# Late expert slots appended to the early slots' chain, and the residual stream's stores moved to another queue and one step later

## The chip, the cores and the metric

The kernel runs on one core of a Trainium2 chip. Its time is the device time of one execution, in microseconds (us). Each core has five engines that run their own instruction streams: TensorE (PE, matmuls), VectorE (DVE), ScalarE (ACT), GpSimd (POOL) and SyncE (SP). Data moves by DMA; a transfer is issued by one of the engines' queues, here mostly the synchronous engine's (SP) and GpSimd's, and all of them share the same 16 DMA engines. An engine takes its instructions in order, so one that waits for a semaphore holds everything behind it on that engine.

## What is computed

The reference is a two-layer decoder over 4 batches of 512 tokens of width 256. The last two stages are what the change touches. Stage five is a cross attention block with its own feed-forward network; stage six is a mixture of experts, 8 experts with 1024 hidden units, of which each token takes the best two:

```python
gate_scores = jax.nn.softmax(x @ Wg + bg, axis=-1)
topk_scores, topk_idx = jax.lax.top_k(gate_scores, TOP_K)
topk_scores = topk_scores / (jnp.sum(topk_scores, axis=-1, keepdims=True) + 1e-08)
...
for e in range(NUM_EXPERTS):
    h = jax.nn.gelu(x @ W1[e] + b1[e])
    y = h @ W2[e] + b2[e]
    output = output + y * combine_w[..., e:e + 1]
```

The input x of this stage is a layer norm of the residual stream, and the stage's output is added to the residual stream.

## The kernel before

**The expert stage.** The kernel does not multiply every token with every expert. For each batch `gate` computes the layer norm, the gate scores and the best two experts, and scatters every token's normalised row (256 values and four more for its weights and its number) to two places in a tensor `rows` in device memory, where each expert has its own region: eight indirect DMAs of 128 rows each, on GpSimd's queue (L1667). It also adds the experts' second biases to the residual stream (`biases2`, VectorE L1687) and, in its last piece, stores that batch of the residual stream to the tensor `sums` (L1689, GpSimd's queue).

The rows of an expert are then worked off in slots of 128 rows; there are 39 slots. For a slot, the synchronous queue loads the 128 rows (`zs`, L1791) and the whole weights of its expert (`we`, 2 MB, L1797). `turn` transposes the rows on TensorE (L1812), copies them on VectorE (`zsT`, L1814) and computes the tokens' numbers (`to`, L1818) and weights (`wts`, L1820 and L1821). `hidden` makes the hidden units in two halves of 16 matmul instructions on TensorE (L1830) and the activations on ScalarE (L1832). `output` multiplies with the second weights (L1837), scales on VectorE (`ys`, L1839) and adds the 128 rows to `sums` with an indirect DMA on GpSimd's queue (L1840). At the very end the kernel copies `sums` to its output (L1878).

`sums` is one tensor to the framework that places the waits, so every access to it, a store of a batch or a scatter-add, waits for the one before. The pool of `to` and `wts` has four buffers, so slot k's `to` waits until the scatter-add of slot k - 4 has landed. The pool of `we` has four buffers too, `ys` has three, `zs` has 16.

**Early and late slots.** After the third of the four batches the first 16 slots (`NEARLY`) can be filled from what has been scattered by then; `count_early` and `table_early` decide which expert and which rows each has. The other 23 need the last batch (`count_late`, `table_late`). So early slots start while the last batch's feed-forward part and gate still run.

**Who sets the order.** Stages two, five and six are laid out by a planner, `Stream`, in steps `s.t`. Its attention tiles have fixed steps. Everything else hangs in chains: lists of pieces, each with the step from which it may be laid, the step by which it must be, a gap in steps, a cost and a function that issues its instructions. `fill` lays pieces of any chain that are ready and for which there is room, the one with the earliest due step first; between chains with the same due step the first in the list goes first. A piece with cost 0 has room always. Once attention's tiles are done, the room is 3.0 a step for each of two kinds of cost.

The early slots are one chain, made by `tail` from `slots.begin` (L1296), due at step 10**6. Its rounds are: fetch slot s + 3 (cost 0), `hidden` of slot s + 1 in two halves (2.0 each), `turn` of slot s + 2 (0.5), `output` of slot s (3.4). A fetch of a slot loads `zs` (late slots only; the early ones' are all loaded at the beginning) and `we`; slot 16 loads `we` first. The late slots are a second chain with the same due step, made by `rest` (L1435) among the gate's pieces of the last batch. Its first piece is the fetch of slot 16, with cost 0, so it is laid as soon as the chain is there, while the early chain's next piece has no room. The emitted order of loads is therefore slots 0 to 8, then 16, then 9 to 15, then 17 and on. The load of slot 16's table entries waits for `table_late`, and that of its `zs` for the last batch's row scatters.

The gate's pieces for batch b are put together in `gate` and made into a chain by `leave` (L1437), which inserts the counts, the tables, and `slots.go` or `rest` at places counted from the list's end.

Of the kernel before, what the change touches and what calls it, by code (L numbers as in the profile page):

```python
# [20 lines left out]
P = 128  # L21
B, T, C = 4, 512, 256
# [18 lines left out]
def decoder_kernel(ctx: ExitStack, tc: tile.TileContext, a: dict, out: bass.AP):  # L41
    nc = tc.nc
    V, G, S, PE = nc.vector, nc.gpsimd, nc.scalar, nc.tensor

    def ts(i, n=P):
        return slice(i * n, (i + 1) * n)

    def mid_bc(ap, n):
        return ap.unsqueeze(1).to_broadcast([ap.shape[0], n, ap.shape[1]])
# [31 lines left out]
    def ring():  # L81
        return banks["s"].tile([P, 512], F32, name="ps_s", tag="s")
# [132 lines left out]
    def add_to(dst, ps):  # L215
        V.tensor_add(dst, ps, dst)
# [93 lines left out]
    class Stream:  # L310
# [22 lines left out]
        def chain(self, items, spill=False):  # L333
            items = [[*i] for i in items]
            for i, j in zip(items[-2::-1], items[:0:-1]):
                i[1] = min(i[1], j[1])
            self.chains.append(SimpleNamespace(items=deque(items), at=-99, spill=spill))

        def lay(self, c):
            cost, fn = c.items.popleft()[3:]  # L340
            c.at = self.t
            fn()
            if not c.items:
                self.chains.remove(c)
            self.spent[cost < 0] += abs(cost)
# [893 lines left out]
    def l1_xattn(cn_d, moe, early):  # L1239
        with early.stack as st:  # L1240
# [25 lines left out]
            def ffn_weights(p, w):  # L1266
                w["li1"] = load(early.pl, "li1", rows(f"{p}_li1"), [P, 4, C])
                w["li2"] = load(early.pl, "li2", rows(f"{p}_li2"), [P, 2, 1024])
                w["li3"] = load(one, "li3", rows(f"{p}_li3"), [P, 8, C])
# [6 lines left out]
            for k in range(2):  # L1276
# [8 lines left out]
            s = Stream(  # L1285
                list(jobs.values()), tail=lambda: tail(), ptp=ptp, ptmp=wk, op=one, qap=qmp, nms=nms, ones=ones, identb=identb,
                onesf=onesf,
            )

            back = set()  # L1290
            slots = Slots(moe, gs)

            def tail():
                if slots.ready:
                    inner.close()
                    s.chain([(s.t + 4, 10**6, 0, c, f) for c, f in slots.begin(st)])  # L1296
                return slots.ready

            def block(k, b):
# [31 lines left out]
                def flip(z, c, outs):  # L1331
                    ps = ring()
                    for t in range(NT):
                        PE.transpose(ps[:, ts(t)], z[:, t, ts(c)], ident)
                    for n, (dst, o) in enumerate(outs):
                        gc, bc = pv[:, o + c : o + c + 1], pv[:, o + 2 + c : o + 3 + c]
                        if n == 0:
                            S.activation(dst[:, c, :], ps, AF.Identity, bias=bc, scale=gc)
                        else:
                            V.tensor_scalar(dst[:, c, :], ps, gc, bc, ALU.mult, ALU.add)  # L1340
# [56 lines left out]
                def mlp():  # L1397
                    def li1(t):
                        ps = ring()
                        for g in range(4):  # L1400
                            PE.matmul(ps[:, 0:C], e.yT[:, g, ts(t)], w["li1"][:, g, :], start=g == 0, stop=g == 3)
                        add_to(e.xo[:, t, :], ps[:, 0:C])

                    def mid():
                        e.nT = one.tile([P, 2, T], F32, name="nT5", tag="nT5")
                        G.tensor_add(x1, x1, e.xo)
                        G.tensor_add(x1, x1, mid_bc(bl3, NT))

                    def li2(f):
                        if f == 0:  # L1410
                            e.h = one.tile([P, 8, T], F32, name="hT5", tag="hT5")
                        ps = ring()
                        for c in range(2):
                            PE.matmul(ps, w["li2"][:, c, ts(f)], e.nT[:, c, :], start=c == 0, stop=c == 1)
                        if f % 2:
                            S.activation(e.h[:, f, :], ps, AF.Identity, bias=pv[:, 12 + f : 13 + f])
                        else:
                            V.tensor_scalar_add(e.h[:, f, :], ps, pv[:, 12 + f : 13 + f])

                    def gelu():  # L1420
                        S.activation(e.h, e.h, AF.Gelu)
                        S.preload_act_table_set("natural_log_exp_and_others")
                        if k:
                            e.kept = one.tile([P, NT, C], F32, name="kept", tag="xo")
                            nc.sync.dma_start(e.kept, kept[b])

                    def li3(t):
                        ps = ring()
                        for f in range(8):
                            PE.matmul(ps[:, 0:C], e.h[:, f, ts(t)], w["li3"][:, f, :], start=f == 0, stop=f == 7)  # L1430
                        add_to(x1[:, t, :], ps[:, 0:C])

                    def rest():
                        s.chain([(s.t, 10**6, 0, c, f) for c, f in slots.rest()])

                    def leave():
                        if k:  # L1437
                            G.tensor_add(x1, x1, e.kept)
                            g = gate(
                                moe, b, SimpleNamespace(), gs,  # L1440
                                lambda: one.tile([P, 2, T], F32, name="hT6", tag="hT6"), ring,
                            )
                            more = {
                                B - 2: [(1, 1.0, slots.count_early), (1, 1.0, slots.table_early)],
                                B - 1: [(1, 1.0, slots.count_late), (1, 1.0, slots.table_late)],
                            }.get(b, [])
                            g[-7:-7] = more
                            if more:
                                g[-3:-3] = [(0, 0.0, rest if b == B - 1 else slots.go)]
                            s.chain([(s.t, s.t + 2 + int(0.7 * i), gap, c, f) for i, (gap, c, f) in enumerate(g)])  # L1450
                        back.add(b)
                        if not k and b == B - 1:
                            ffn_weights("a2", ws[1])

                    t0 = s.t
                    work = [(True, 1.7, lambda: li1(0))] + [(False, 1.7, lambda t=t: li1(t)) for t in range(1, 4)]
                    work += [(1, -1.2, p) for p in ln_pieces(e.xo, z3)]
                    work += [(0, 0.0, mid), (True, 0.5, lambda: flip(e.z3, 0, [(e.nT, 8)]))]
                    work += [(False, 0.5, lambda: flip(e.z3, 1, [(e.nT, 8)]))]
                    work += [(f == 0, 1.7, lambda f=f: li2(f)) for f in range(8)]  # L1460
                    work += [(True, 0.0, gelu)]
                    work += [(t == 0, 3.4, lambda t=t: li3(t)) for t in range(4)]
                    work += [(False, 0.0, leave)]


                    lag, pace = {(0, 0): (1, 1.0), (0, B - 1): (3, 1.1), (1, B - 2): (2, 0.65)}.get((k, b), (3, 1.0))
                    s.chain([
                        (t0, t0 + (1 if i < 4 else lag + int(pace * (i - (i > 8)))), gap, c, f)
                        for i, (gap, c, f) in enumerate(work)
                    ])  # L1470
# [17 lines left out]
                for g in range(4):  # L1488
                    u = jobs[k, b, g]
                    u.done = lambda o, g=g: finish(g, o)  # L1490
                    f = u.first_d
# [79 lines left out]
    def gate(m, b, e, gs, hT, bank):  # L1571
        xb = x[:, ts(b, NT), :]
# [91 lines left out]
        def scatter(t):  # L1664
            for k in range(2):
                i = b * NT + t
                G.indirect_dma_start(  # L1667
                    m.rows, bass.IndirectOffsetOnAxis(ap=m.idx[:, i, k : k + 1], axis=0), e.zr[:, t, :], None
                )
# [13 lines left out]
        def biases2(h):  # L1683
            ps = bank()
            for t in range(2):
                PE.matmul(ps[:, ts(t, C)], e.cT[:, ts(2 * h + t)], m.b2, start=True, stop=True)
            V.tensor_add(xb[:, ts(h, 2), :], ps.rearrange("p (t c) -> p t c", c=C), xb[:, ts(h, 2), :])  # L1687
            if h:
                G.dma_start(m.sums[ts(b, T), :].rearrange("(t p) c -> p t c", p=P), xb)  # L1689

        return (
            [(2 if i == 0 else 1, -1.2, p) for i, p in enumerate(ln_pieces(xb, z))]
# [1 line left out]
            + [(1, -1.5, choose), (1, -1.2, choose2), (1, -1.2, choose3), (1, 0.5, rank)]  # L1694
            + [(t == 0, 0.0, lambda t=t: scatter(t)) for t in range(NT)]
            + [(1, 0.7, biases), (1, 0.9, lambda: biases2(0)), (0, 0.9, lambda: biases2(1))]
        )


# [312 lines left out]
```

## Time and profile before

| what | us |
|---|---|
| median of 3 runs | 3479.34 |
| lowest and highest run | 3470.84 and 3481.77 |
| the profiled execution's own time | 3483.41 |
| its span | 3481.7 |
| TensorE busy | 3066.6 (88%) |
| VectorE busy | 2092.8 (60%) |
| ScalarE busy | 1902.4 (55%) |
| GpSimd busy | 815.4 (23%) |
| DMA moved | 174.52 MB, mean 50 GB/s |
| first and last scatter-add issued | 3110.4 and 3468.3 |

Times in the profile count from the span's start. A row such as `we<-in_we` names the tile that is written and what it is read from; a line number is that of the kernel before. In a timeline, a row gives the start, the duration, the engine, the line, the operation with its tiles, how many instructions it merges, and in square brackets how long the engine sat idle before it and what released it. DMA rows on GpSimd's queue show the issue, not the landing. SPq is the synchronous engine's queue. In the waits, a row gives the waiting engine and tile, what it waited for, the total in us, how many times, and the longest.

### The profile page before, as it was taken

The numbers are of one execution on the slowest core, as the hardware profiler recorded it, in microseconds if no ns is written. First come the engines' busy times: TensorE is split into PE (matmuls) and PEld (weight loads), VectorE is DVE, ScalarE is ACT, GpSimd is POOL, SyncE is SP. The second block draws the span as 40 slices with busy tenths as digits, with TensorE's granted clock in tenths as the row PEclk, the third lists the DMA queues.
The fourth block names the chain that finished last, engine by engine and source line by source line (L and its number), as shares of the span: only waits on it lengthen the run. The fifth ranks groups of instructions, "written<-read, shape, count | busy, mean of one in ns | idle before, by whom it ended". The sixth has DMA issues, their size and how long they took to land. (4 is left out here: it accounts for less than half of the span.)

```text
span 3481.7 us, 50606 instructions
## 1 busy us (share of the span) xinstructions
PE 3066.6 (88%) x19095; PEld 1497.5 (43%) x19095; DVE 2092.8 (60%) x5138; ACT 1902.4 (55%) x3845; POOL 815.4 (23%) x679
## 2 busy tenths in 40 slices
PE   6689999999998666677899999999999998987997
PEld 3433333334334344344434444433333333447896
DVE  4576676777765687876676565665746646433111
ACT  2225555454554764779588676556663664542221
POOL 1010112122022745668212121100101201122111
PEclk9889999999999567777799999999998999999998
DMA  9100000010001100120000000000000000045896
GB/s 287 55 28 7 1 7 3 6 31 4 10 19 42 49 6 32 37 86 7 25 1 1 1 4 16 7 1 31 13 1 5 21 1 13 13 172 172 288 310 190
DMA packets 78405, 174.52 MB, mean 50 GB/s; under 512 B 5640, under 2 KB 61200, under 8 KB 72976
## 3 DMA queue, kind: packets, MB, share of 16 engines
q1 hardware_dynamic: 68304, 155.47, 12.9%
q0 software_dynamic: 7728, 11.47, 1.5%
q10 hardware_dynamic: 2128, 4.34, 0.3%
q8 instruction: 150, 2.46, 0.3%
q14 instruction: 95, 0.78, 0.1%
HBM read 125.46 MB, written 47.90 MB: 50 GB/s over the span
## 5 line engine op out<-in xcount | busy, mean ns | idle before, releaser
L426 ACT ACTIVATE pt<-ps_s 128x512 f32<-128x512 f32 (+2 forms) x1536 | 792.1, 569 | 744.8 <-PE ps_s L425 649.6
L390 PE MATMUL ps_s<-kT,qT 32*128 32x512 f32 (+3 forms) x3072 | 923.0, 623 | 45.7 <-ACT pt L426 27.9
L402 DVE TENSOR_REDUCE mx<-ps_s 128x1 f32<-128x512 f32 x768 | 489.7, 684 | 221.7 <-PE ps_s L390 123.2
L390 PEld LDWEIGHTS ps_s<-kT,qT 32*128 32x128 f32 x3072 | 309.8, 186 | 338.8 <-issue 96.9
L394 DVE TENSOR_REDUCE mx<-ps_s 128x1 f32<-128x512 f32 x512 | 328.5, 685 | 193.4 <-PE ps_s L390 190.1
L425 PE MATMUL ps_s<-qa,kT 32*128 32x512 f32 (+3 forms) x1536 | 440.5, 588 | 4.5 <-ACT pt L426 3.1
L425 PE MATMUL ps_s<-qT,kT 32*128 32x512 f32 x1536 | 418.6, 638 | 0.0
L406 ACT ACTIVATE ps_s<-ps_s,mx 128x512 f32<-128x512 f32 x512 | 340.8, 670 | 27.5 <-DVE mx L394 27.0
L1832 ACT ACTIVATE hid<-ps_s,we 128x128 f32<-128x128 f32 x312 | 88.9, 368 | 236.4 <-issue 146.1
L1109 POOL TENSOR_TENSOR s<-s,mh 128x1280 f32<-128x1280 f32 x64 | 186.7, 2942 | 81.9 <-ACT mh L1108 64.1
L398 DVE CUSTOM_DVE_ANT_0 junk<-ps_s,dmask 128x256 f32<-128x256 f32 (+3 forms) x256 | 125.6, 491 | 92.0 <-PE ps_s L425 40.3
L1830 PE MATMUL ps_s<-zsT,we 128*128 128x128 f32 x1248 | 153.6, 283 | 26.6 <-DMA we<-in_we 14.8
L167 POOL TENSOR_TENSOR ln_r<-ln_ve,mhalf 128x4 f32<-128x4 f32 x40 | 40.8, 1020 | 532.5 <-DVE ln_ve L162 468.7
L1830 PEld LDWEIGHTS ps_s<-zsT,we 128*128 128x128 f32 x1248 | 150.9, 199 | 32.4 <-issue 17.1
L425 PEld LDWEIGHTS ps_s<-qa,kT 32*128 32x128 f32 x1536 | 143.3, 184 | 47.3 <-DVE mx L402 23.9
L1092 PE MATMUL ps_s<-qk 32*128 32x256 f32 (+3 forms) x512 | 103.2, 609 | 67.2 <-DVE mh L1097 56.5
L418 PE MATMUL ps_s<-qm,all 3*128 3x512 bf16 x768 | 156.9, 388 | 5.9 <-ACT ps_s L406 3.1
L1124 POOL TENSOR_TENSOR s<-s 128x1280 f32<-128x1280 f32 x64 | 147.6, 2337 | 12.3 <-ACT s L1120 12.3
L1151 DVE COPY pt<-ps_s 128x512 f32<-128x512 f32 x160 | 108.4, 688 | 62.0 <-PE ps_s L1149 62.0
L1149 PE MATMUL ps_s<-ident,s 128*128 128x128 f32 x640 | 130.5, 341 | 16.5 <-ACT s L1143 15.3
L1837 PE MATMUL ps_s<-we,hid 128*128 128x256 f32 x624 | 141.7, 381 | 0.0
L1097 DVE TENSOR_SCALAR_CACHE_REDUCE mh<-ps_s 128x512 f32<-128x512 f32 (+3 forms) x256 | 108.5, 487 | 51.7 <-PE ps_s L1096 27.4
(435 smaller groups left out, 5155.1 us busy)
## 6 DMA issues: line engine op xcount, KB each, us to landing
we<-in_we SPq DMA_DIRECT2D x39, 2052.0 KB, 9.1
rows<-zero SPq DMA_DIRECT2D x8, 2080.0 KB, 19.1
qk_d<-qkT SPq DMA_DIRECT2D x32, 256.0 KB, 2.5
qk<-qk_d SPq DMA_DIRECT2D x8, 1024.0 KB, 6.2
zs<-rows SPq DMA_DIRECT2D x39, 130.0 KB, 8.8
li<-in_a_li SPq DMA_DIRECT2D x4, 1024.0 KB, 5.5
v_d<-vp SPq DMA_DIRECT2D x16, 143.5 KB, 1.8
v<-v_d SPq DMA_DIRECT2D x4, 574.0 KB, 6.8
```

The source lines that it names most:

```text
L390: PE.matmul(ps[:, 0:n], u.qT[r, ts(qt)], u.kT[r, hf * 512 : hf * 512 + n], start=True, stop=True)
L394: V.tensor_reduce(m, ps[:, 0:n], AX.X, ALU.max, negate=True)
L402: V.tensor_reduce(m, ps[:, 0:n], AX.X, ALU.max)
L406: S.activation(ps, ps, AF.Exp, bias=m, accum_out=sm)
L418: PE.matmul(ps, self.ones[r, :], u.qm[r, :], start=True, stop=False)
L425: PE.matmul(ps[:, c0:], u.kT[r, ts(kt)], (u.qa if u.first_row else u.qT)[r, c0:], start=u.first_row, stop=True)
L426: S.activation(u.pt[:, j, c0:], ps[:, c0:], AF.Exp, scale=u.scale)
L1109: G.tensor_add(s, s, m)
L1124: G.tensor_mul(s, s, s)
L1149: PE.transpose(ps[:, ts(j)], u.s[h // 2][:, h % 2, c0 : c0 + P], ident)
L1830: PE.matmul(ps[:, ts(f)], u.w[:, k : k + P], u.zT[:, c, :], start=c == 0, stop=c == 1)
L1837: PE.matmul(ps[:, 0:C], u.h[:, f, :], u.w[:, 2048 + f * C : 2048 + f * C + C], start=f == 0, stop=f == 7)
```

## The change

Two things are changed. First, `rest` no longer makes a chain of its own. `Stream.chain` returns the chain that it makes, `tail` keeps it, and `rest` appends the late slots' pieces to it, so that they are laid after the early ones; if the early chain has already run empty, it is put back in the planner's list. Second, the store of a batch of the residual stream is taken out of `biases2` and becomes a piece of its own, `store`, one step later at the earliest. For batches 0 to 2 the synchronous queue issues it; for the last batch GpSimd does, as before. The places that `leave` counts from the list's end are moved by one, so that what it inserts stands where it stood.

```diff
@@ Stream.chain
             self.chains.append(SimpleNamespace(items=deque(items), at=-99, spill=spill))
+            return self.chains[-1]
@@ l1_xattn: tail
                 if slots.ready:
                     inner.close()
-                    s.chain([(s.t + 4, 10**6, 0, c, f) for c, f in slots.begin(st)])
+                    slots.chain = s.chain([(s.t + 4, 10**6, 0, c, f) for c, f in slots.begin(st)])
@@ l1_xattn: block, mlp
                     def rest():
-                        s.chain([(s.t, 10**6, 0, c, f) for c, f in slots.rest()])
+                        c = slots.chain
+                        if not c.items:
+                            s.chains.append(c)
+                        c.items.extend([s.t, 10**6, 0, cost, f] for cost, f in slots.rest())
@@ leave
-                            g[-7:-7] = more
+                            g[-8:-8] = more
                             if more:
-                                g[-3:-3] = [(0, 0.0, rest if b == B - 1 else slots.go)]
+                                g[-4:-4] = [(0, 0.0, rest if b == B - 1 else slots.go)]
@@ gate
             V.tensor_add(xb[:, ts(h, 2), :], ps.rearrange("p (t c) -> p t c", c=C), xb[:, ts(h, 2), :])
-            if h:
-                G.dma_start(m.sums[ts(b, T), :].rearrange("(t p) c -> p t c", p=P), xb)
+
+        def store():
+            (nc.sync if b < B - 1 else G).dma_start(m.sums[ts(b, T), :].rearrange("(t p) c -> p t c", p=P), xb)
...
             + [(1, 0.7, biases), (1, 0.9, lambda: biases2(0)), (0, 0.9, lambda: biases2(1))]
+            + [(1, 0.0, store)]
```

In the emitted order, TensorE, VectorE and ScalarE have the same instructions in the same order as before. GpSimd's queue loses the three stores of batches 0 to 2. The synchronous queue gains them: batch 0's stands between the load of `kept` for batch 0 and the context load (`cn`) of batch 3, batch 1's between the loads of `kept` for batches 1 and 2, batch 2's between the last early `zs` load and slot 3's weights. Slot 16's `we` and `zs` loads stand behind slot 15's `we`.

## The prediction

> **What bounds the kernel now.** I read the page first. TensorE is busy for 88% of the span, but the chain that ended last is not TensorE's: it is one DMA after another.
>
> ```profile
> span 3481.7 us, 50606 instructions
> DMA sums<-ys,to 5%; DVE wts L1821 0%; DVE to L1818 0%; DVE wts L1820 0%; POOLq L2008 0%; DVE ys L1839 0%; POOLq L1840 0%
> sums<-ys,to POOLq DMA_INDIRECT x39, 6.5
> ```
>
> These are the 39 scatter-adds of the expert slots, each adding 128 rows into `sums`. GpSimd issues each one only when the one before has landed. The waits confirm it. The `to` cast of a slot sits on VectorE until the scatter four slots earlier has landed, 30 times, and TensorE's wait for expert weights is small beside that.
>
> ```profile
> DVE to L1818 <- DMA sums<-ys,to: 176.8, 30, 10.3
>   DMA we<-in_we: 14.8, 4
> ```
>
> The second line comes from the view of the tile `we`: four waits of TensorE for weights, 14.8 us in all. I then read the timelines of the tail, GpSimd's first, then TensorE's and the synchronous queue's.
>
> ```profile
> 3208.99 1.61 POOL L1840 DMA_INDIRECT sums<-ys,to  x1 [0.30 <-issue]
> 3214.01 0.84 POOL L1689 DMA_DIRECT2D sums<-x  x1 [3.41 <-DVE wts L1821]
> 3227.36 1.60 POOL L1840 DMA_INDIRECT sums<-ys,to  x1 [12.51 <-DMA sums<-x]
> ...
> 3281.91 1.54 POOL L1840 DMA_INDIRECT sums<-ys,to  x1 [7.50 <-DVE wts L1821]
> ...
> 3362.62 1.54 POOL L1840 DMA_INDIRECT sums<-ys,to  x1 [5.01 <-DVE wts L1821]
> 3371.28 1.54 POOL L1840 DMA_INDIRECT sums<-ys,to  x1 [7.11 <-DVE wts L1821]
> ...
> 3449.01 1.54 POOL L1840 DMA_INDIRECT sums<-ys,to  x1 [5.27 <-DVE wts L1821]
> 3455.00 1.56 POOL L1840 DMA_INDIRECT sums<-ys,to  x1 [4.45 <-DVE ys L1839]
> ...
> 3468.34 1.54 POOL L1840 DMA_INDIRECT sums<-ys,to  x1 [2.94 <-DMA sums<-ys,to]
> ```
>
> The reader sees a chain without a gap from 3209 to the end, and three step lengths. While weights stream at an even pace, 3281.91 to 3362.62 is 11 steps of 7.34 us. Where TensorE stalls and the weight loads come in pairs, 3371.28 to 3449.01 is 9 steps of 8.64. With no weights left, 3455.00 to 3468.34 is 3 steps of 4.45.
>
> ```profile
> 3206.96 3.62 PE L1837 MATMUL ps_s<-we,hid 128*128 128x256 f32 x16
> 3221.54 5.56 PE L1830 MATMUL ps_s<-zsT,we 128*128 128x128 f32 x32 [10.96 <-DMA we<-in_we]
> ...
> 3382.73 5.21 PE L1830 MATMUL ps_s<-zsT,we 128*128 128x128 f32 x32 [2.55 <-DVE zsT L1814]
> ```
>
> ```profile
> 3194.11 0.34 SPq L1797 DMA_DIRECT2D we<-in_we  x1
> 3210.22 0.34 SPq L1791 DMA_DIRECT2D zs<-rows  x1
> 3211.41 1.51 SPq L1797 DMA_DIRECT2D we<-in_we  x2
> ```
>
> TensorE's largest weight wait, 10.96 us, comes from this queue. The load at 3194.11 is slot 16's, the first late slot, issued ahead of slots 9 to 15. Behind it the same slot's `zs` holds the queue until the last batch's row scatters have landed (3210.22), and slot 9's weights start at 3211.41.
>
> **The change part by part.** The profiled execution took 3483.41 us around its span of 3481.7, 0.12% above the median of 3479.34. I work the sum as a difference and apply it to the median.
>
> *Stores of batches 0 to 2 move from GpSimd to the synchronous queue.* Off GpSimd come three issues of 0.82 to 0.84 us and their waits. Batch 0's had no wait and idle time behind it: nothing. Batch 1's held GpSimd for 18.84 us for VectorE's L1687, with L1406 and L1407 behind it. Those feed the third output matrix of that block and the load of `kept` (2966.12), whose reader L1438 starts at 3033.13, so nothing again; without that cover it would be up to 19 us. Batch 2's stood in front of work that TensorE waited for:
>
> ```profile
> 3083.68 0.82 POOL L1689 DMA_DIRECT2D sums<-x  x1
> 3084.52 2.35 POOL L1378 TENSOR_TENSOR xo<-x,bc 128x1024 f32<-128x1024 f32 x1
> ...
> 3087.33 8.22 PE L1401 MATMUL ps_s<-li,yT 128*128 128x256 f32 x26 [7.48 <-POOL yT L1390]
> ```
>
> So `xo`, `yT` and the last block's first output matrix come 3084.52 - 3083.68 = 0.84 us earlier. The gain lies between 0 (a later wait swallows it) and 0.84; nothing in the last block runs beside it as an alternative path, so I take 0.84.
>
> On the synchronous queue the three stores have this cost. Batch 0's now waits for L1687 at 2713 ahead of the context load of batch 3, which went out at 2512.37. That load moves to about 2716, lands in 4.8 us (the median of its row), and its first reader is the key matmul at 2768.8: 48 us of cover. Batch 1's stands ahead of `kept` and is ready at 2963, before that load's own 2966. Batch 2's goes behind the 13 `zs` loads (3113.84) and ahead of slot 3's weights. It delays those by one issue, about 1.1 us by the queue's spacing, but they land near 3124 and TensorE reads them at 3150.76. The first scatter-add must now wait for this store: 3114.9 plus the row's 4.5 us is 3119.4, not 3110.41. Behind it on GpSimd stands L1438 at 3148.07, which waits 36.02 us for VectorE: 28 us of cover. All nothing. Batch 3's store keeps its place on GpSimd between the same two scatter-adds, so its 12.51 us wait stays unless the traffic around it changes.
>
> *Late slots in the early chain.* No instruction is added or removed, and TensorE's, VectorE's and ScalarE's order is unchanged. Slot 16's weights and `zs` move behind slot 15's on the synchronous queue. Slot 9's load goes out at 3194.1; slots 10 and 11 follow outputs 6 and 7 (about 3203.4 and 3210.6). All four weight buffers then serve the next slots, not three. All four weight waits, 14.8 us, should go, with the slow matmuls after the long one (5.56 against 3.73 us): 14.8 + 1.8 = 16.6 us for TensorE.
>
> How much of that reaches the end? TensorE may lead the scatter-adds by about five slots only: slot k's weights meet `zsT` k, which stands on VectorE behind the `to` cast that waits for scatter k-5. The chain was already back to back. So the gain must come from shorter scatter steps. In the stretch up to the scatter of 3227.36 I take nothing. The rows scatters and the scatter at 3208.99 lose a quiet stretch (a rows scatter beside a load took 3202.15 - 3194.42 = 7.73 us, one without 2.73: up to +5, and the scatter-add up to 7.34 - 4.45 = +2.9). The store loses its double load (12.6 us to landing against a median of 4.5: up to -8.1). The bounds nearly cancel, 7.9 against 8.1. After it, weights are ahead: by 3212.6 both versions have issued 12 loads, but the next goes out at 3230.80 now, and then about 3218 (slot 9 starts at 3210.4, where slot 7's output ends, and slot 8's output ends one period of 7.25 later). One to two loads finish earlier, so one to two more scatters run at 4.45 and not 7.34: 2.9 to 5.8 us. I take the middle, 4.4. The ends are 16.6 of gain (all of TensorE's time returns) and the loss worked out in the rivals.
>
> [...]
>
> Sum: -0.84 - 4.4 = -5.2 us, or 3474 on the median.
>
> **The rivals.** *TensorE's time returns whole.* In the even stretch a scatter step, 7.34, is only 0.1 us over TensorE's own period (3278.59 to 3285.84, 7.25). If the early lead in weights lets scatters land in less than that, the backlog dissolves and TensorE sets the end: -16.6 - 0.84 = -17.4, 3462. Against it: the 30 waits at L1818.
>
> *Slower: the paired regime starts early.* If TensorE meets the scatter limit from slot 10 or so, weight loads bunch behind its stalls, a scatter issued late in a load lands only when the next load ends, and steps take 8.64 in place of 7.34. In the trace this began at slot 25, when a scatter started 5.55 us after a weight load (3371.28 against 3365.73; before that 3.1 to 4.8). From slot 10, 15 more steps of 1.3 us are +19.5 - 0.84 = +18.7, 3498. It decides if five or more extra steps (+6.5) beat the 5.2 gained.
>
> *The reordering does nothing.* The scatter chain hides all weight waits and only 0.84 us remains: 3478.5.
>
> **How the numbers follow.** My forecast, gaining 2 to 10 us, has 0.41; TensorE's time back 0.27; nothing 0.14; paired regime 0.18. Within 0.3% is 10.4 us, about what a measurement of this kernel can tell. Of the forecast 0.07 lies beyond it, and of the second rival 0.25 does: faster 0.32. Of the paired regime 0.16 lies beyond the bound, with 0.02 for a cover above that fails: slower 0.18. Same is the rest, 0.50. The range reaches below the first rival by 3 us and up to most of the slow one: 3459 to 3492. The forecast's own range is 3469 to 3477.
>
> **What would show it.** Right: no `we` wait at slot 9, weight issues at 3194, 3203 and 3211 with the first late slot's after slot 15's, `xo` directly behind the rows scatters at 3083.7, and four or five scatter steps near 4.4 at the end in place of three. Wrong: `to` waits well under 176.8 us with TensorE unbroken (first rival), or more waits of TensorE for `zsT` and more steps over 8 us (the slow one). A wait for `cn` at 2768, or a scatter chain that starts well after 3209, would say that a cover I named is gone.

## The result and the profile after

| kernel | runs | median us | lowest to highest |
|---|---|---|---|
| before | 14 | 3479.98 | 3467.82 to 3490.90 |
| changed | 14 | 3482.77 | 3466.78 to 3513.23 |

The ratio of the times is 1.0017, 95% interval 0.9993 to 1.0042: no change that a measurement of this kernel can tell. The forecast of "no change" held, and 3482.77 lies in the range given. But the middle of the forecast, 3474, was 9 us too low, and its difference of -5.2 us, a ratio of 0.9985, lies below the interval. So "no change" is in part luck. The profiles show that the gap is not chance alone: one step of the sum has the wrong sign.

The profiled execution of the changed kernel took 3479.9 us around a span of 3478.2. First the waits:

```profile
DVE to L1825 <- DMA sums<-ys,to: 193.0, 30, 17.9
```

No wait of TensorE for `we` is left in the changed kernel. The four of 14.8 us in all are gone, as forecast. The waits of the `to` cast for scatter-adds have grown from 176.8 to 193.0 us. The tail on GpSimd, in the order of the timeline (the scatter-adds are L1847 now, the row scatters L1672, the store L1695):

```profile
3200.91 0.97 POOL L1672 DMA_INDIRECT rows<-gz,idx  x1 [2.07 <-DMA rows<-gz,idx]
3207.93 0.97 POOL L1672 DMA_INDIRECT rows<-gz,idx  x1 [6.05 <-DMA rows<-gz,idx]
3214.98 0.97 POOL L1672 DMA_INDIRECT rows<-gz,idx  x1 [6.09 <-DMA rows<-gz,idx]
3216.27 1.60 POOL L1847 DMA_INDIRECT sums<-ys,to  x1 [0.32 <-issue]
3225.33 0.83 POOL L1695 DMA_DIRECT2D sums<-x  x1 [7.45 <-DVE wts L1828]
3234.96 1.61 POOL L1847 DMA_INDIRECT sums<-ys,to  x1 [8.80 <-DMA sums<-x]
...
3446.61 1.54 POOL L1847 DMA_INDIRECT sums<-ys,to  x1 [5.10 <-DVE wts L1828]
3451.07 1.54 POOL L1847 DMA_INDIRECT sums<-ys,to  x1 [2.92 <-DVE wts L1828]
3455.53 1.54 POOL L1847 DMA_INDIRECT sums<-ys,to  x1 [2.92 <-DMA sums<-ys,to]
3460.42 1.54 POOL L1847 DMA_INDIRECT sums<-ys,to  x1 [3.35 <-issue]
3464.64 1.54 POOL L1847 DMA_INDIRECT sums<-ys,to  x1 [2.68 <-DMA sums<-ys,to]
```

Three things are to be seen. The last row scatters stand 7 us apart, not 2.7, and the scatter-add in front of the store takes 9.06 us from issue to the store's issue. They now run beside the weight loads of slots 9 to 11, issued at 3199.11, 3208.47 and 3215.61, which in the kernel before still waited (slot 9's went out at 3211.41). So the scatter-add behind the store goes out 49.2 us after the batch's first row scatter (3185.74), against 44.7 us before (3182.67 to 3227.36): 4.5 us lost. Before, one row scatter was slow (7.73 us) and the scatter-add took 5.02. And the remaining 32 steps take 229.7 us (3234.96 to 3464.64), against 241.0 (3227.36 to 3468.34): 11.3 us won, with four short steps at the end where there were three. TensorE now waits for `zsT`, which stands on VectorE behind the `to` cast:

```profile
3225.99 6.64 PE L1837 MATMUL ps_s<-zsT,we 128*128 128x128 f32 x32 [3.17 <-DVE zsT L1821]
3245.09 5.67 PE L1837 MATMUL ps_s<-zsT,we 128*128 128x128 f32 x32 [8.78 <-DVE zsT L1821]
3299.31 3.84 PE L1837 MATMUL ps_s<-zsT,we 128*128 128x128 f32 x32 [1.19 <-DVE zsT L1821]
3310.18 5.47 PE L1837 MATMUL ps_s<-zsT,we 128*128 128x128 f32 x32 [3.36 <-DVE zsT L1821]
```

That is 16.5 us of waiting in four pieces. The kernel before had, beside its four weight waits, three waits of this kind near the end. The first, of 2.55 us, stands in the prediction; these are the others:

```profile
3402.03 5.47 PE L1830 MATMUL ps_s<-zsT,we 128*128 128x128 f32 x32 [2.99 <-DVE zsT L1814]
3422.52 5.46 PE L1830 MATMUL ps_s<-zsT,we 128*128 128x128 f32 x32 [4.00 <-DVE zsT L1814]
```

So the waits for `zsT` grew from 9.5 to 16.5 us. Of the 14.8 us that TensorE gained, the scatter-adds took back 7.0 in this pair of profiles.

The last finding lies far ahead of the tail, where the stores were moved. These are the timelines of the kernel before near 2943, of GpSimd, VectorE, ScalarE and TensorE (the same columns as in the prediction):

```profile
2942.98 1.04 POOL L167 TENSOR_TENSOR ln_r<-ln_ve,mhalf 128x4 f32<-128x4 f32 x1
2944.06 0.16 DVE L172 TENSOR_TENSOR ln_t<-ln_r 128x4 f32<-128x4 f32 x1 [4.79 <-POOL ln_r L167]
2944.45 0.17 DVE L174 TENSOR_SCALAR ln_t<-ln_t 128x4 f32<-128x4 f32 x1
2946.28 0.66 ACT L406 ACTIVATE ps_s<-ps_s,mx 128x512 f32<-128x512 f32 x1 [4.37 <-DVE mx L394]
2947.11 2.08 PE L1360 MATMUL ps_s<-cn,wk 128*128 128x512 f32 x2 [3.58 <-ACT ps_s L406]
2962.86 0.84 POOL L1689 DMA_DIRECT2D sums<-x  x1 [18.84 <-DVE x L1687]
2963.72 2.37 POOL L1406 TENSOR_TENSOR x<-x,xo 128x1024 f32<-128x1024 f32 x1
```

And the same place in the changed kernel:

```profile
2941.99 1.04 POOL L167 TENSOR_TENSOR ln_r<-ln_ve,mhalf 128x4 f32<-128x4 f32 x1
2943.02 2.33 POOL L1407 TENSOR_TENSOR x<-x,xo 128x1024 f32<-128x1024 f32 x1
2943.07 2.31 DVE L172 TENSOR_TENSOR ln_t<-ln_r 128x4 f32<-128x4 f32 x1 [3.98 <-POOL ln_r L167]
2945.43 2.35 POOL L1408 TENSOR_TENSOR x<-x,bc 128x1024 f32<-128x1024 f32 x1
2945.61 2.20 DVE L174 TENSOR_SCALAR ln_t<-ln_t 128x4 f32<-128x4 f32 x1
2949.47 0.66 ACT L407 ACTIVATE ps_s<-ps_s,mx 128x512 f32<-128x512 f32 x1 [7.74 <-DVE mx L395]
2950.30 2.07 PE L1361 MATMUL ps_s<-cn,wk 128*128 128x512 f32 x2 [6.93 <-ACT ps_s L407]
```

Before, batch 1's store held GpSimd for 18.84 us. Now GpSimd goes on at once to two large adds, and they fall on a layer norm of VectorE. Two instructions of 128x4 elements that took 0.16 and 0.17 us take 2.31 and 2.20, each until GpSimd's add has ended. Behind them on VectorE stand the maxima (`mx`) that ScalarE and then TensorE wait for: TensorE's idle time before the key matmul grows from 3.58 to 6.93 us, 3.35 us lost.

The last block of the changed kernel shows the rest of the stores' effect:

```profile
3089.70 8.66 PE L1402 MATMUL ps_s<-li,yT 128*128 128x256 f32 x26 [6.64 <-POOL yT L1391]
3134.45 16.68 PE L1431 MATMUL ps_s<-li,hT 128*128 128x256 f32 x64 [3.70 <-ACT hT L1422]
```

The sum of the moved stores in this pair of profiles: +3.35 at the key matmul; -0.84 at `xo` (TensorE's wait for `yT` fell from 7.48 to 6.64 us); +0.44 in the 26 matmuls behind that wait (8.66 us, before 8.22); +0.91 in the 64 matmuls of the last block's third matrix (16.68, before 15.77, behind a wait of 3.7 us in both). That is +3.86. TensorE was 0.17 us earlier before that place (the matmul of L1679 at 2937.95, now L1684 at 2937.78) and is 3.65 us later at an expert matmul behind that block (3154.41 against 3150.76): 3.82.

### The profile page after: what moved, and what is told of

It is laid out like the page before. It is cut to its first block, busy times and chain, and to the rows that moved or that the text cites. A ratio compares the mean times of both kernels' runs of the same rounds, so it can differ in the third digit from the quotient of the medians.

```text
span 3478.2 us, 50606 instructions
## 1 busy us (share of the span) xinstructions
PE 3066.9 (88%) x19095; PEld 1497.6 (43%) x19095; DVE 2096.2 (60%) x5138; ACT 1903.2 (55%) x3845; POOL 813.2 (23%) x676
## 5 line engine op out<-in xcount | busy, mean ns | idle before, releaser
L1839 ACT ACTIVATE hid<-ps_s,we 128x128 f32<-128x128 f32 x312 | 89.1, 369 | 229.7 <-issue 181.2
```

## The experiments

Each execution has an offset of its own from the first part of the kernel, up to some 6 us (VectorE's instruction of L172 near 2943 starts at 2940.48 in one profile and at 2946.12 in another, both with the moved stores), so the places below are compared by idle times and durations, not by start times. The edits of the first two kernels are the two halves of the change.

**The chain alone.** The kernel before with only this:

```diff
+            return self.chains[-1]
...
+                    slots.chain = s.chain([(s.t + 4, 10**6, 0, c, f) for c, f in slots.begin(st)])
...
+                        c.items.extend([s.t, 10**6, 0, cost, f] for cost, f in slots.rest())
```

> The kernel before with the chain edit alone: late slots' pieces appended to the early chain, stores left as they were. Theory (the serial scatter-adds set the end, and weight waits lie behind them): no weight wait of TensorE is left (14.8 us before), yet the time stays within 0.3% of before, 3475 to 3488, and the first scatter-add after the last batch's store starts later after that batch's row scatters than before (44.7 us from the first row scatter to it in the profile before, about 49 here). Rival (the two parts cancel: the chain edit gives TensorE's 16.6 us back and the stores cost as much): 3463, 0.5% faster.

Measured: 3474.38 us (3464.91 to 3491.43, 12 runs), ratio 0.9992 (0.9971 to 1.0012). The weight waits are gone here too, and the waits for `zsT` are 22.2 us, 12.7 more than before. The scatter-add behind the store comes 48.8 us after the first row scatter (4.1 lost), and the last one at 3462.43, 236.6 us later (4.4 won against 241.0). The loss and the gain cancel within the tail. In the changed kernel's profile they left a gain of 6.8 us.

**The stores alone.** The kernel before with `store` and the moved places of `leave`, and `rest` as it was.

> The kernel before with the stores' edit alone: batches 0 to 2 stored by the synchronous queue a step later, slot 16 still fetched ahead of slot 9. Theory: 0.8 us faster at most, the wait of TensorE for yT after the third batch falls from 7.5 to about 6.6 us, and the four weight waits stay (14 to 15 us); time within 0.3% of before. Rival (the parts cancel): 0.5% slower, about 3496, with a new wait behind one of the stores on the synchronous queue.

Measured: 3486.72 us (3475.13 to 3495.38, 12 runs), ratio 1.0013 (0.9996 to 1.0029). The 0.84 us are there (`yT` wait 6.61), but the run is no faster: the two slow VectorE instructions are there as well (2.31 and 2.20), and TensorE's idle time before the key matmul is 7.26 us. The profiled execution, 3494.83 us, also shows the slow regime of the prediction's rival in a kernel that has the old chain: from 3294.89 to 3457.32 it makes 18 scatter steps of 9.02 us on average. So that regime belongs to the serial scatter-adds beside weight loads, and not to the new order. Five steps of 4.2 to 4.8 us follow at the end, with the old chain.

**Half of the scatter-adds.** Both kernels without the scatter-adds of odd slots, so half of the experts' sums are missing. The edit in both:

```diff
-            G.indirect_dma_start(
+            if u.s % 2 == 0:
+                G.indirect_dma_start(
```

> The kernel before with the scatter-adds of the odd slots left out, so 20 of 39 remain and half of the experts' outputs are missing from the result. Theory: with half as many serial scatter-adds TensorE sets the end of the tail; its waits for zsT (about 14 us with the slow matmuls after them) go, its weight waits (14.8 us) stay: 3459 to 3468. Rival (scatter-adds are no bound): within 0.1% of before.

> The changed kernel with the scatter-adds of the odd slots left out in the same way. Theory: with the scatter chain out of the way the removed weight waits show in full: 12 to 17 us below the same cut of the kernel before, 3444 to 3454. Rival (the removed waits were worth nothing to TensorE either, for instance because loads only wait elsewhere): equal to the cut of the kernel before within 3 us.

Measured: 3458.77 us (3456.96 to 3461.42, 5 runs), ratio 0.9939 (0.9917 to 0.9962), for the kernel before; 3452.65 us (3446.74 to 3453.04, 4 runs), ratio 0.9916 (0.9888 to 0.9943), for the changed one. The serial scatter-adds do set the end: with half of them the kernel before is 20 us faster, and the changed one lies 26 us below the whole kernel before. In the waits of the first, GpSimd now waits for TensorE's results and not the reverse:

```profile
POOL sums L1841 <- DVE ys L1839: 237.1, 19, 16.3
```

The distance of the two kernels was a miss: 6.1 us. The weight waits are time of the end here (13.8 us in the profile of the first), so more was expected. The changed kernel had a new wait of 4.02 us, behind slow row scatters:

```profile
3202.47 0.97 POOL L1672 DMA_INDIRECT rows<-gz,idx  x1 [5.78 <-DMA rows<-gz,idx]
3210.69 0.97 POOL L1672 DMA_INDIRECT rows<-gz,idx  x1 [7.25 <-DMA rows<-gz,idx]
3218.50 0.97 POOL L1672 DMA_INDIRECT rows<-gz,idx  x1 [6.84 <-DMA rows<-gz,idx]
...
3235.49 5.46 PE L1837 MATMUL ps_s<-zsT,we 128*128 128x128 f32 x32 [4.02 <-DVE zsT L1821]
```

With its slow matmuls (5.46 against 3.73) that is 5.8 us. The rest of the gap is the cost of the moved stores, as in the pair above: 3.8 at the key matmul (7.38 us idle against 3.59), 2.6 at the 64 matmuls (16.64 against 14.08), less 0.8 at `yT` (6.47 against 7.26), and 0.3 in the matmuls behind it (8.61 against 8.32), 5.9 in all. The weight waits with the slow matmuls behind the first (6.42) come to 16.5; 16.5 - 5.8 - 5.9 = 4.8, near the 6.1 measured.

**Deeper buffers.** Both kernels with more buffers for what the scatter-adds read, so that TensorE can run further ahead of them:

```diff
-            self.yp = pool(stack, "l6y", 3)
+            self.yp = pool(stack, "l6y", 7)
+            self.op = pool(stack, "l6o", 12)
...
-            u.to = self.tp.tile([P, 1], I32, name="to", tag="to")
+            u.to = self.op.tile([P, 1], I32, name="to", tag="to")
...
-            u.wt = self.tp.tile([P, 1], F32, name="wts", tag="wts")
+            u.wt = self.op.tile([P, 1], F32, name="wts", tag="wts")
```

> The changed kernel with 12 buffers instead of four for the token numbers `to` and weights `wts`, and seven instead of three for `ys`, so that `to` no longer waits for the scatter-add four slots earlier and TensorE may run about eight slots ahead of the scatter-adds. Theory: the serial scatter-adds set the end, and their steps are long because weight loads run beside them. TensorE then works through the 30 slots after 3210 at 7.25 us each, without a wait for `zsT`, its last weight load lands some 20 us earlier, and about three more scatter steps take 4.45 us in place of 7.34: 8.7 us less than the changed kernel, and the run-to-run spread becomes smaller if the stalls for `zsT` are its cause. Rival: the 33 scatter steps take the same time whatever TensorE does; then within 3 us of the changed kernel.

> The kernel before with the same deeper buffers. Theory: it still has its four waits for weights (14.8 us) and slot 9's gap, so TensorE's end lies about 15 us later than in the changed kernel with deep buffers; by the step lengths 4.45 and 7.34 that is two scatter steps or 5.8 us later than that one, and some 5 us below the kernel before. If the change's reordering is worth something only while TensorE may run ahead, the distance between the two deep kernels is larger than the distance between the two plain ones, which is none. Rival: the two deep kernels are alike within 3 us, because the waits for weights are hidden by the scatter chain however deep the buffers are.

Measured: 3473.91 us (3466.98 to 3488.75, 12 runs), ratio 0.9981 (0.9962 to 1.0), and 3474.37 us (3468.7 to 3482.5, 12 runs), ratio 0.9981 (0.9966 to 0.9997). In the profile of the changed kernel with deep buffers TensorE waits for no `zsT` in the tail, as expected, and its last matmuls begin at 3427.33. But the scatter-adds go on to 3456.32, one behind the other:

```profile
3424.86 1.54 POOL L1847 DMA_INDIRECT sums<-ys,to  x1 [2.98 <-DVE ys L1846]
3429.32 1.54 POOL L1847 DMA_INDIRECT sums<-ys,to  x1 [2.92 <-DMA sums<-ys,to]
3433.74 1.54 POOL L1847 DMA_INDIRECT sums<-ys,to  x1 [2.88 <-DMA sums<-ys,to]
...
3456.32 1.54 POOL L1847 DMA_INDIRECT sums<-ys,to  x1 [2.80 <-DMA sums<-ys,to]
```

The two deep kernels are alike, although the kernel before with deep buffers still shows its `we` wait of 9.17 us. By itself that is the rival's result. But the changed one carries its stores' cost, some 5 us as above, so by estimate the chain is worth about that much here, near the 5.8 of the theory. No run had the new chain and the deep buffers with the stores as before. In this pair of profiles, the way from the last batch's first row scatter to the last scatter-add is 9.4 us shorter in the changed kernel (271.4 and 280.8), while TensorE's last matmul, counted from the same scatter, ends 16.3 us earlier. So the scatter chain hides a good part of TensorE's gain also with these buffers.

**No weight loads.** The changed kernel, in which slots 4 to 38 load no weights and use those of slots 0 to 3:

```diff
         def fetch_w(self, u):
+            if u.s > 3:
+                u.w = self.us[u.s % 4].w
+                return
```

> The changed kernel without the weight loads of slots 4 to 38: they multiply with the weights of slots 0 to 3, so the result is another one. Theory: without loads beside them the last batch's row scatters stand 2.7 us apart throughout, the store lands in about 4.5 us, and a scatter-add step of 4.45 us is shorter than TensorE's 7.25 us period, so the scatter chain is bound by TensorE and not the reverse: no 30 waits of `to`, the steps 7.25 us, the end some 25 us earlier, 3450 to 3457. Rival: the steps of 7.3 us and more are the scatter-adds' own, with loads or without; then the chain and the time stay within 5 us of the changed kernel.

Measured: 3451.76 us (3447.49 to 3452.43, 3 runs), ratio 0.991 (0.9879 to 0.9941). The eight row scatters stand 2.7 to 3.5 us apart, the store lands in under 4.4 us (3207.83 to the next issue at 3212.22), and from 3232.53 on the scatter-adds follow TensorE at its own 7.25 us:

```profile
3207.83 0.84 POOL L1695 DMA_DIRECT2D sums<-x  x1 [3.36 <-DVE wts L1831]
3212.22 1.61 POOL L1850 DMA_INDIRECT sums<-ys,to  x1 [3.55 <-DMA sums<-x]
...
3232.53 1.53 POOL L1850 DMA_INDIRECT sums<-ys,to  x1 [4.17 <-DVE ys L1849]
3239.77 1.53 POOL L1850 DMA_INDIRECT sums<-ys,to  x1 [5.71 <-DVE ys L1849]
```

The long steps are therefore the weight loads' doing. With the loads beside it, a scatter-add is as slow as TensorE's whole slot (7.34 us in the even steps of the kernel before, against 7.25).

**Two tensors for the sums.** The changed kernel with a second, zeroed tensor for the odd slots 7 to 35, so that two scatter-adds may be under way:

```diff
+        m.sums2 = dram.tile([B * T + P, C], F32, name="sums2", tag="sums2")
...
+            other = u.s % 2 and 5 < u.s < NSLOT - 2
             G.indirect_dma_start(
-                self.m.sums, bass.IndirectOffsetOnAxis(ap=u.to, axis=0), y, None, compute_op=ALU.add
+                self.m.sums2 if other else self.m.sums, bass.IndirectOffsetOnAxis(ap=u.to, axis=0), y, None, compute_op=ALU.add
...
+            for b in range(B):
+                V.tensor_add(part[b], x[:, ts(b, NT), :], part[b])
+                qs[b % 2].dma_start(view(out[b]), part[b])
```

> The changed kernel with a second, zeroed tensor `sums2` that takes the scatter-adds of the odd slots 7 to 35; the last copy becomes two loads, an add on VectorE and a store. The result is the whole one. Theory: two chains of half the length are no longer the bound, TensorE sets the end as in the changed kernel with half the scatter-adds (3452.65 median), and the longer end costs 6 to 8 us (512 KB loads of about 6 us in place of nothing, and an add): 3457 to 3463, with a spread under 8 us, against 3479 of the kernel before. Rival: the DMA work itself is the limit, both scatter-adds slow each other to twice the step, and the time is 3480 or more.

Measured: 3473.59 us (3464.84 to 3480.96, 12 runs), ratio 0.9983 (0.9965 to 1.0001). A miss by 10 us and more. The steps of the tail were TensorE's 7.25 us from 3257 to 3452, as expected. But `to` kept its four buffers, so around the store TensorE stood for `zsT` as before (3.69 and 10.08 us, and slow matmuls behind both). The expectation had taken these waits for part of the long chain. They come from the buffers of `to`, as the next runs show. The longer end took 19.0 us from the last scatter-add's issue, against 13.6 in the changed kernel.

**Both together, in both orders of the chain.** `sums2` and the deep buffers, in the changed kernel and in the kernel before.

> The changed kernel with both earlier edits: `sums2` for the odd slots 7 to 35, and 12 buffers for `to` and `wts`, seven for `ys`. The result is the whole one. With `sums2` alone TensorE still stood 3.69 + 10.08 us for `zsT`, behind `to` casts that waited for the scatter-adds around the store, and its next 32 matmuls took 5.47 and 6.39 us instead of 3.73: 18.2 us in all. With the deep buffers alone those waits were gone. Theory: TensorE now sets the end and works without a wait from 3194 on, so 18.2 us less than with `sums2` alone: 3455, 3452 to 3459, and a spread under 10 us. Rival: something else ends last once TensorE runs free (`ys` buffers or the loads of weights), and the time is 3465 or more.

> The kernel before with the same two edits. It tells what the change is worth once the scatter-adds no longer set the end. Theory: TensorE's four waits for weights (14.8 us in the trace of before) and the slow matmuls behind the long one (1.8) are now time of the end, with the 0.84 us of the moved store: 16 to 18 us slower than the changed kernel with the same edits, near 3472. Rival: the waits for weights are hidden by something else than the scatter-adds, and the two are alike within 4 us, as the two kernels with deep buffers alone were.

Measured: 3457.39 us (3454.4 to 3462.82, 9 runs), ratio 0.9941 (0.9919 to 0.9962), and 3469.23 us (3466.43 to 3472.71, 12 runs), ratio 0.998 (0.9965 to 0.9994). Now the two differ by 11.8 us, where the plain ones and the deep ones did not. In the tail of the first, behind the gate, TensorE has one wait, 0.23 us. These are the second one's, of TensorE's timeline:

```profile
3219.96 6.21 PE L1832 MATMUL ps_s<-zsT,we 128*128 128x128 f32 x32 [11.01 <-DMA we<-in_we]
3238.66 3.81 PE L1832 MATMUL ps_s<-zsT,we 128*128 128x128 f32 x32 [1.57 <-DMA we<-in_we]
3254.45 3.81 PE L1832 MATMUL ps_s<-zsT,we 128*128 128x128 f32 x32 [0.96 <-DMA we<-in_we]
3262.41 3.81 PE L1832 MATMUL ps_s<-zsT,we 128*128 128x128 f32 x32 [0.47 <-DMA we<-in_we]
3270.34 3.81 PE L1832 MATMUL ps_s<-zsT,we 128*128 128x128 f32 x32 [0.45 <-DMA we<-in_we]
```

They sum to 14.5 us, and the slow matmuls behind the first to 2.5: 17 us, what the new chain removes. The difference fell 5 us short of it. The first kernel's moved stores account for that: 3.6 at the key matmul (7.01 us idle, 3.39 in the second), 2.6 at the 64 matmuls near 3133 (16.67 and 14.08), less 0.9 at `yT` (6.61 and 7.49), and 0.4 behind it (8.65 and 8.28), 5.7 in all, so 11.3.

**One store back.** The changed kernel with both edits, and batch 1's store put back to where the kernel before has it:

```diff
+            if h and b == 1:
+                G.dma_start(m.sums[ts(b, T), :].rearrange("(t p) c -> p t c", p=P), xb)

         def store():
-            (nc.sync if b < B - 1 else G).dma_start(m.sums[ts(b, T), :].rearrange("(t p) c -> p t c", p=P), xb)
+            if b != 1:
+                (nc.sync if b < B - 1 else G).dma_start(m.sums[ts(b, T), :].rearrange("(t p) c -> p t c", p=P), xb)
```

> The changed kernel with `sums2` and the deep buffers, and batch 1's store alone put back where the kernel before has it, on GpSimd's queue in `biases2`. The result is the whole one. In the traces of all seven kernels with the moved stores, everything after 2943 runs 3.4 us later than in the five without: GpSimd, no longer held by that store, runs `x<-x,xo` and `x<-x,bc` (2.33 and 2.35 us) just when VectorE has two 0.16 us instructions of a layer norm, and these take 2.31 and 2.20 us. Theory: with the store back GpSimd is held again, both instructions of VectorE take 0.16 us, TensorE's idle time before the key matmul at 2947 is 3.6 us and not 6.9, and the time is 3.4 us less than with all stores moved: about 3454. The 0.84 us at `xo` of the last block stays. Rival: the two slow instructions have another cause (the synchronous queue's store, which is in this kernel for batches 0 and 2): then they stay at 2.2 us or more and the time stays near 3457.

Measured: 3455.17 us (3452.04 to 3457.86, 6 runs), ratio 0.9928 (0.9903 to 0.9953). The trace decides, since 2.2 us between two chips is near what the runs can tell:

```profile
2943.65 0.16 DVE L172 TENSOR_TENSOR ln_t<-ln_r 128x4 f32<-128x4 f32 x1 [4.16 <-POOL ln_r L167]
2944.04 0.17 DVE L174 TENSOR_SCALAR ln_t<-ln_t 128x4 f32<-128x4 f32 x1
2946.70 2.07 PE L1361 MATMUL ps_s<-cn,wk 128*128 128x512 f32 x2 [2.94 <-ACT ps_s L407]
2962.77 0.85 POOL L1696 DMA_DIRECT2D sums<-x  x1 [19.16 <-DVE x L1694]
2963.65 2.38 POOL L1407 TENSOR_TENSOR x<-x,xo 128x1024 f32<-128x1024 f32 x1
```

GpSimd is held again, the instructions are short again, and TensorE's idle time is 2.94 us. Batches 0 and 2 still go by the synchronous queue, and batch 1's own went out only at 2965.85 in the changed kernel, so it is not that queue's stores that made VectorE slow.

**All stores back.** The kernel before with the new chain, `sums2` and the deep buffers.

> The kernel before with the late slots appended to the early chain, `sums2` and the deep buffers, and all four stores as in the kernel before. The result is the whole one. Theory: it has TensorE's unbroken tail and not the 3.4 us at 2943; it loses the 0.84 us at `xo`. In the traces the kernels with the old stores had gained a further 1.7 to 2.6 us at the third output matrix of the last block near 3135 (64 matmuls in 14.1 or 15.8 us, not 16.7, after the same 3.7 us wait). So 3452 to 3455, and 15 to 18 us under the kernel before with the same two edits (3469.23). Rival: the stores' edit is worth nothing by itself, and the time is that of the changed kernel with the two edits, 3457.4, within 1.5 us.

Measured: 3452.77 us (3446.09 to 3454.54, 6 runs), ratio 0.9921 (0.9895 to 0.9946). This is the best version found, 0.8% below the kernel before. Its 64 matmuls near 3130 take 14.08 us, those of the kernel with one store back 16.62.

The rows that tell the stores apart, over all 14 profiles:

| stores | kernels | idle before key matmul | wait for `yT` | 64 matmuls near 3133 |
|---|---|---|---|---|
| as before | 6 | 3.14 to 3.59 | 7.26 to 7.49 | 14.08, once 15.77 |
| batch 1's as before | 1 | 2.94 | 7.14 | 16.62 |
| moved | 7 | 6.84 to 7.38 | 6.47 to 6.65 | 16.64 to 16.72, without weight loads 14.08 |

## Where the prediction held and where it failed

**What bounds the kernel: held.** Halving the scatter-adds took 20 us, the changed kernel without most weight loads lay 31 below (0.991 of 3480), and two tensors with deep buffers handed the end to TensorE.

**The weight waits: held, and so did their being worth little.** All 14.8 us went, and the waits for `zsT` grew by 7.0 us in the changed kernel and by 12.7 with the chain alone. That the first rival, TensorE's time returned whole, did not come is shown by the two deep kernels (alike, by estimate some 5 us apart without the stores' cost) beside the two with `sums2` as well (11.8 us apart, and 16.5 with all stores as before). The mechanism was that rival's; what was missing was the condition that scatter-adds must not set the end.

**"In the stretch up to the scatter of 3227.36 I take nothing": wrong in size.** The bounds were 7.9 of loss and 8.1 of gain. It measured +4.5 us in the changed kernel and +4.1 with the chain alone. In the changed kernel the loss was whole, 4.2 us at the row scatters and 4.0 at the scatter-add. The gain at the store was mis-sized, 3.7 in place of 8.1: it still took 9.63 us from its issue to the next scatter-add's (3225.33 to 3234.96), since weight loads ran beside it here too (one issued at 3222.86; the DMA engines' share was 0.77 from 3215 to 3235). Before, it took 13.35.

**"I take the middle, 4.4": met by the chain alone, but not confirmed.** The steps behind the store gave 4.4 us there and 11.3 in the changed kernel, so that the first meets the forecast to the tenth is luck. Four short steps at the end, not three, came in the changed kernel. But the stores alone have five, with the old chain, and the chain alone has three in a row. Over the whole stretch there are 5 and 6 steps under 5 us with the old chain, 7 and 8 with the new one; that would be the one to two more of the forecast, though some lie far from the end. And such a stretch of 32 steps took 229.7, 236.6, 241.0 and 250.6 us in the four profiles of kernels with the plain tail, and the last two share the old chain. One profiled pair can't size a term of a few us here.

**"Batch 1's held GpSimd for 18.84 us ... so nothing again": the step that failed.** I asked who waits for GpSimd's L1406 and L1407 and found nobody, which was right. I did not ask what these two adds would run beside once they came 20 us earlier. The loss of 3.35 us was outside the bounds, which were nothing and a loss of cover. In the trace the multiply at L172 takes 2.31 us in place of 0.16 and ends 0.03 us after GpSimd's first add. The next one at L173 goes through in 0.16 us at 2945.41, just before the second add begins at 2945.43. The instruction at L174, which starts at 2945.61, takes 2.20 us in place of 0.17 and ends 0.03 us after the second add. All seven kernels with the moved stores have 2.31, 0.16 and 2.20 us at these three lines, the seven with batch 1's store as before 0.16, 0.16 and 0.17. By what rule the two instructions waited, no run here shows.

**The 0.84 us: held, and outweighed.** The wait for `yT` fell by just that. Half of it went in slower matmuls behind it.

**The covers on the synchronous queue: held.** `cn` went out at 2714.77 with no wait at its reader, and the first scatter-add at 3120.59 after 12.84 us, with nothing late behind it.

**The paired regime: not tied to the change.** It appeared in the profile of the stores alone, with the old chain. The changed kernel had 10 steps over 8 us behind the store, the kernel before 12. My reason, that an earlier lead in weights would start it, is not supported.

So the forecast was met by another path than its own. The stores' loss of 4 to 6 us is shown by the idle times of all profiles and, where TensorE sets the end, by 4.6 us between the runs (3457.39 and 3452.77); 3.4 us of it is explained above, the part at the 64 matmuls is not. The chain's gain in the kernels with the plain tail is not sized: from the last batch's first row scatter to the last scatter-add, the new chain is shorter by 0.3 us (the chain alone against before), 6.8 (changed against before) and 17.0 (changed against the stores alone). The runs of the two halves, 0.9992 and 1.0013, both have 1 in their intervals. That a gain of some 5 us by the chain and the stores' loss cancel, and not, as forecast, that a gain of 5 us is too small to be seen, is the likeliest reading; the runs of the plain kernels can't prove it.

## What to carry to other kernels

When a wait is taken off an engine, look not only for who waits for its next instructions but for what they will run beside: two adds of GpSimd (2.33 and 2.35 us) each made an instruction of VectorE on TensorE's path, of 0.16 and 0.17 us, last until the add had ended (2.31 and 2.20 us). A removed stall is worth its time only where its engine sets the end; here the same reordering gave nothing that the runs could tell beside a serial chain of scatter-adds, and 16.5 us once a second tensor and a few more small buffers had ended that chain. Ask too what a chain of small transfers will run beside: the hole in the weight stream that this change closed had been carrying the last row scatters and a scatter-add, and filling it cost them 8.2 us.

## What the runs showed that I had not expected

- **Spread.** Kernels whose end is set by scatter-adds beside loads vary by 14 to 46 us from run to run. Those whose end TensorE sets vary by 4.5 to 8.5 us (half of the scatter-adds, no loads, two tensors with deep buffers), with 3 to 12 runs each. At 12 runs the range was 6.3 us for the kernel before with two tensors and deep buffers, 13.8 with the deep buffers alone. How the scatter-adds fall between the loads seems to be the cause, since its steps range from 4.4 to 11.6 us within one profile (the chain alone); it was not tested by itself. With two tensors alone the spread was 16 us.
- **Small transfers beside a load.** From one issue to the next, a row scatter took 2.7 us alone and up to 8.6 beside weight loads (the stores alone), a scatter-add 4.4 and up to 11.6 (the kernel before with deep buffers), the 512 KB store 4.4 (without weight loads) and up to 13.4 (the kernel before).
- **The same wait, three prices.** TensorE's wait of 3.70 or 3.71 us for `hT` was followed by 64 matmuls in 14.08, 15.77 or 16.6 to 16.7 us. In the changed kernel (16.68 us) the granted clock was 0.53 from 3135 to 3140, with the chain alone (14.08 us) 1.00 throughout, from 3120 to 3145. In the table above all seven kernels with batch 2's store moved and with the weight loads in place paid the highest price. What sets it stays open.
